# A copy ahead of the recurrent layer's gather, three places a step for the next chunks' stages, and a later final norm, in a four-layer graph network

## The chip, the cores and the metric

One core of a Trainium2 chip runs the whole kernel. Its engines are PE (TensorE: matrix products, with its weight loads shown apart as PEld), DVE (VectorE), ACT (ScalarE), POOL (GpSimd) and SP (SyncE, which issues nearly all transfers here). The metric is the device time of one execution in microseconds; less is better.

## The reference, cut to what matters

There are 128 graphs of 64 nodes with 256 features. Four layers follow one another, each as a residual and a layer norm over the features: `x = layernorm(x + layer(x))`.

- Layer 0 runs graph convolutions on five groups of the first 25 nodes.
- Layer 1 is one normalised graph convolution, layer 2 a polynomial of degree 3 in the row-normalised adjacency.
- Layer 3 is a gated recurrent unit that is stepped five times over the graph:

```python
A = (adj != 0).astype(x.dtype)
h = x
for l in range(5):
    m = einsum('bnd,de->bne', h, weight[l])
    agg = einsum('bij,bid->bjd', A, m)
    h = gru_cell(agg, h, w_ih, w_hh, b_ih, b_hh)
```

with `r` and `z` two sigmoid gates, `n = tanh(i_n + r * h_n)` and `h = (1 - z) * n + z * h`. All of it is float32. The change is in layer 3 and in how the work of layers 1 and 2 is laid between its steps.

## The kernel before, in words

The graphs are cut into 16 chunks of 8 graphs: four pairs of graphs, 128 rows each, so a chunk's state is 128 rows by 4 pairs by 256 features (`xt`), and transposed (`hT`, `hn`) 128 features by 2 halves by 512 nodes.

**Layer 3's main loop (L1011 to L1050)** has 80 steps, of which the last is written out by itself. Two chunks take turns: an even step belongs to one, an odd step to the other, and a chunk gets five steps, one for each application of the unit. Ten steps make a round of two chunks; the text counts them t=0 to t=9. There are eight rounds. In a step `x` is the chunk whose gates are computed and `w` is the other chunk, stepped just before. The order of PE's instructions is the order of the source (`manual_schedule` for PE alone). The other engines' orders are set by a scheduler from the dependencies, with `high_priority` for some instructions; each engine then works its list in order.

In a step PE computes the two big gates (r and z) in seven products `rz(1)` to `rz(7)`, and the candidate in seven products `n(1)` to `n(7)`; this is a product scheme of seven instead of eight (class `Gates`, L744 to L788). Each `rz` product is 8 instructions and each `n` product 4, in the lines of L759. Products 1, 6, 7 and 4 accumulate in one bank `a` (`parz`, `pan`); after 1, 6 and 7 ACT copies the bank to a tile `c` (L776), and the next product of the same bank waits for that copy. Products 5, 7 and 3 use a bank `d` (`pdrz`, `pdn`), and DVE adds `d` and a copy (L778, L788). The order in a step is: rz 1, 2, 6; filler; rz 5, 7; n 1, 2; rz 4; n 6; rz 3; n 5; filler; n 7; gather of `w`; n 4; n 3.

**The gather** (`messages`, L811, and `gather`, L206 to L215) multiplies, for each half k of the features, each pair's 128 by 128 state as the weights with the 0/1 adjacency `A01` as the moving operand, into a bank `pa`; ACT copies the bank to `agg` (L214), and POOL forms sums of it (`sums`, L736). For a chunk's first application the weights come from `xt`, where features are consecutive. For the four others they come from `h`.

**How `h` comes about** (`flip`, L862 to L880): DVE transposes each half of the new state in 32 by 32 blocks to a tile `flip` (L870), SP stores it to device memory (`hb`, L873) and loads it back in four transfers (L878) to `h`, a tile of 128 rows by 256 features by 4 pairs. The pair is the innermost index there, so consecutive features of one pair are 16 bytes apart: `src = lambda q, k: h[:, k * 128 : (k + 1) * 128, q]` (L815). `h` has one buffer.

**`close`** (L971 to L991): for `w` after its gather place, it counts the layer up and calls `messages`; after the fifth application it adds `h` to `xt` (DVE, L986), norms `xt` (DVE statistics, POOL power, ACT apply at L149) and stores it (SP, L991). When a chunk ends, a new chunk `nxt` is taken in: two transposes of its state (L800, L807) and its first gather.

**The filler** is the generator `mid` (L220 to L322), which computes layers 1 and 2 of the two chunks of the next round in stages. Each `next(filler)` runs one stage: S1 adjacency masks and sums (DVE); S2 four transposes (L259); S3 a product `pp` (L270), a gather `ag1` of 16 instructions and a second product (L278); S4 16 products `pd` with the layer-1 weights (L288) and statistics; S5 the norm (L152); S6 a gather `ag2`; S7 16 products with the layer-2 weights (L309), activation and statistics; S8 the norm. There are two places a step (L1027 after rz 6, L1041 after n 5), so the 16 stages of two chunks fill t=0 to t=7.

Of the kernel before, what the change touches and what calls it, by code (L numbers as in the profile page):

```python
# [9 lines left out]
F32 = mybir.dt.float32  # L10
# [5 lines left out]
B, N, D, HID, L = 128, 64, 256, 512, 5  # L16
# [9 lines left out]
H = CB * N // 2  # L26
NCH = B // CB
NP = CB // 2
# [40 lines left out]
def gnn_stack(  # L69
# [26 lines left out]
    nc = tc.nc  # L96
# [57 lines left out]
    def layernorm(y, by="v", n=NP, r=128):  # L154
        norm_apply(y, *norm_stats(y, by, n, r), by, n, r)
# [20 lines left out]
    def psum(name):  # L176
        return pt.tile([128, 512], F32, tag="pt", name=name)

    def psum0(name):

        taken[0] += 1
        if taken[0] % 8 < 5:
            return pg.tile([128, 512], F32, tag="pg", name=name)
        return psum(name)


    def load_adj(c):
        a64 = keep.tile([128, NP, N], F32, name="a64", bufs=2)
        nc.sync.dma_start(a64, av[c])
        adjs[c] = a64  # L190
# [11 lines left out]
    def halves(x):  # L202

        return lambda q, k: x[:, q, k * 128 : (k + 1) * 128]

    def gather(src, m, name, pool=keep, tag="ag", bufs=1):  # L206

        a = pool.tile([128, 2, NP * 128], F32, tag=tag, name=name, bufs=bufs)
        for k in range(2):
            p = psum("pa")  # L210
            for q in range(NP):
                nc.tensor.matmul(p[:, q * 128 : (q + 1) * 128], src(q, k), m[:, q, :], start=True, stop=True)  # L212
            with tc.high_priority():
                nc.scalar.copy(a[:, k, :], p)  # L214
        return a  # L215
# [1 line left out]
    adjs, xts = {}, {}  # L217
    state = {}

    def mid(c):  # L220

        a64 = adjs.pop(c)

# [33 lines left out]
        p = psum("pT1").rearrange("p (q n) -> p q n", q=NP)  # L257
# [10 lines left out]
        p = psum("pp").rearrange("p (q n) -> p q n", q=NP)  # L268
# [3 lines left out]
        with tc.high_priority():  # L272
            nc.vector.scalar_tensor_tensor(poly, dg, cw[:, 1:2], p, op0=ALU.mult, op1=ALU.add)
        ag = gather(halves(xt), AT1, "ag1")
        nc.vector.tensor_add(xt, xt, l1bs[:, None, :].to_broadcast([128, NP, D]))
        p = psum("pp").rearrange("p (q n) -> p q n", q=NP)
        for q in range(NP):
# [5 lines left out]
        for u in range(NP // 2):  # L283
            p = psum("pd").rearrange("p (q d) -> p q d", q=2)
            for h in range(2):
                q = 2 * u + h
# [4 lines left out]
            for h in range(2):  # L291
                q = 2 * u + h
# [11 lines left out]
        for u in range(NP // 2):  # L304
            p = psum("pd").rearrange("p (q d) -> p q d", q=2)
            for h in range(2):
                q = 2 * u + h
# [5 lines left out]
            for h in range(2):  # L313
                q = 2 * u + h
# [9 lines left out]
    def both(*gens):  # L324
        for g in gens:
            yield from g
# [8 lines left out]
    with ExitStack() as c0:  # L335
        w0 = c0.enter_context(tc.tile_pool(name="w0", bufs=1))
        work = c0.enter_context(tc.tile_pool(name="work0", bufs=1))
# [216 lines left out]
        p = psum0("pw")  # L554
# [27 lines left out]
                    )  # L582
            return p

        early = both(mid(0), mid(1))

        places = [(1, 1), (1, 2), (2, 1), (2, 2), (2, 2), (3, 1), (3, 2), (3, 2)]
        places += [(4, 0), (4, 0), (4, 1), (4, 2), (4, 2), (5, 1), (5, 2), (5, 2)]
# [105 lines left out]
    work = ctx.enter_context(tc.tile_pool(name="work", bufs=1, reuse_waits="tile"))  # L694
# [41 lines left out]
    def sums(a, name):  # L736

        t = work.tile([128, 4, H], F32, tag="T" + name, name="T" + name, bufs=2)
        nc.gpsimd.tensor_sub(t[:, 0:2, :], a[:, :, H:], a[:, 0, :].rearrange("p (s n) -> p s n", s=2))  # L739
        nc.gpsimd.tensor_sub(t[:, 2, :], a[:, 1, H:], t[:, 0, :])  # L740
        nc.gpsimd.tensor_sub(t[:, 3, :], a[:, 1, :H], t[:, 2, :])
        return t

    class Gates:  # L744
# [22 lines left out]
        def product(self, i):  # L767
            C = self.C
            if i == 1:
                self.a = self.bank("a")  # L770
            if i in (1, 6, 7, 4):
                self.multiply(self.a, i)
                if i != 4:
                    c = self.copies[i] = work.tile([128, 2, H], F32, tag="copy", name=f"c{i}", bufs=4)
                    with tc.high_priority():
                        nc.scalar.copy(c, self.a)  # L776
                if i == 7:
                    nc.vector.tensor_add(C[:, :, 1, H:], self.d, self.copies.pop(7))  # L778
            elif i == 2:
                b = self.bank("b")  # L780
                self.multiply(b, i)
                nc.vector.tensor_add(C[:, :, 0, :H], b, self.copies.pop(1))
            else:
                if i == 5:
                    self.d = self.bank("d")
                self.multiply(self.d, i)
                if i == 3:
                    nc.vector.tensor_add(C[:, :, 0, H:], self.d, self.copies.pop(6))  # L788

    class Chunk:  # L790
# [20 lines left out]
        def messages(self):  # L811
            src = halves(self.xt)
            if self.l:
                h = self.h
                src = lambda q, k: h[:, k * 128 : (k + 1) * 128, q]  # L815
            self.agg = gather(src, self.A01, "agg", work, "agg", 2)
            self.ta = sums(self.agg, "a")

# [43 lines left out]
        def flip(self, j):  # L862

            if self.c == NCH - 2 and self.l == L - 1:
                return
            if j:
                self.hb = dram.tile([2, 128, NP * 128], F32, name="hb", bufs=2)
            with tc.high_priority():
                t = work.tile([128, NP, 32, NP], F32, name="flip", bufs=2)
                nc.vector.transpose(  # L870
                    t.rearrange("p r f q -> p q r f"), self.hn[:, j, :].rearrange("p (q r f) -> p q r f", q=NP, r=NP)
                )
                nc.sync.dma_start(self.hb[j], t.rearrange("p r f q -> p (r f q)"))  # L873
                if not j:
                    self.h = work.tile([128, D, NP], F32, name="h", bufs=1)
                    hv = self.hb.rearrange("j (a i) (r c) -> r i (j a) c", i=32, r=NP)
                    for r in range(NP):
                        nc.sync.dma_start(  # L878
                            self.h[32 * r : 32 * (r + 1)].rearrange("p (a f) q -> p a (f q)", f=32), hv[r]
                        )  # L880

        def reset(self, j, f, i, h):
            n, r = self.NI[:, 1], self.RZ[:, 0]
            nc.vector.scalar_tensor_tensor(n[:, j, f], h, bhh[:, 4 + j : 5 + j], r[:, j, f], op0=ALU.add, op1=ALU.mult)  # L884
            nc.vector.tensor_add(n[:, j, f], i, n[:, j, f])  # L885
# [83 lines left out]
                )  # L969

        def close(self, norm=None):  # L971
            self.l += 1
            if self.l < L:
                self.messages()
                return
            if norm:
                mv, rs, _ = norm
                nb = small.tile([128, NP], F32, name="nb")
                nc.vector.scalar_tensor_tensor(nb, mv[:, :, 0], -1.0, rs, op0=ALU.mult, op1=ALU.mult)
                with tc.issue_after(tanhs[-1].ins):  # L980
                    norm_apply(self.xt, mv, rs, nb, "a")
            else:
                for q in range(NP):
                    m = self.c * NP + q
                    y = self.xt[:, q, :]
                    nc.vector.scalar_tensor_tensor(  # L986
                        y, self.h[:, :, q], mask[:, m : m + 1], y, op0=ALU.mult, op1=ALU.add
                    )
                layernorm(self.xt, "a")
            for h in range(2):  # L990
                nc.sync.dma_start(ov[self.c][:, 2 * h : 2 * h + 2], self.xt[:, 2 * h : 2 * h + 2])  # L991
# [4 lines left out]
    rows = []  # L996
# [13 lines left out]
    filler = iter(())  # L1010
    for s in range(NCH * L):  # L1011
        u, t = s // (2 * L) * 2, s % (2 * L)
        if t == 0:
            for _ in filler:
                pass
            if u + 2 < NCH:
                for c in (u + 2, u + 3):
                    load_adj(c)
                    load_x(c)
                filler = both(mid(u + 2), mid(u + 3))  # L1020
        if s == NCH * L - 1:
            break
        x, w = rows[s % 2], before
        nxt = None
        for i in (1, 2, 6):
            x.rz(i)
        next(filler, None)  # L1027
        x.rz(5)
        x.rz(7)
        x.n(1)  # L1030
        x.n(2)
        if w and w.l == L - 1 and w.c + 2 < NCH:
            nxt = Chunk(w.c + 2)
            nxt.state_of_layer2(1)
        x.rz(4)
        if nxt:
            nxt.state_of_layer2(0)
        x.n(6)
        x.rz(3)
        x.n(5)  # L1040
        next(filler, None)  # L1041
        x.n(7)
        if w:
            w.close()
            if nxt:
                nxt.messages()
                rows[(s + 1) % 2] = nxt
        x.n(4)
        x.n(3)
        before = x  # L1050

    x, w = rows[1], before
# [83 lines left out]
```

## Time and profile before

| what | value |
|---|---|
| median of three runs (lowest, highest) | 2286.38 us (2285.2, 2288.13) |
| the profiled execution's own time | 2285.78 us |
| its span in the trace | 2284.0 us |
| granted TensorE clock | 0.997 |
| PE busy | 2237.1 us, 98% of the span |
| weight loads busy | 1965.4 us, 86% |
| DVE, ACT, POOL busy | 1575.7, 953.2, 611.1 us |

The profiled execution is 2 us longer than its span, and 0.6 us under the median of the runs. Layer 3's loop takes the time from about 355 us to the end. PE is busy almost without a gap, so the time is the sum of PE's instructions plus a few waits. Engines other than PE matter where PE waits for them. Rows named L759 with tiles `parz`, `pan`, `pdrz`, `pdn`, `pbrz`, `pbn` are the gate products, rows L212 with `pa` the gathers. In a timeline, instructions of one line that follow each other are merged to one row with a count; a bracket names the idle time before it and what ended it.

### The profile page before, as it was taken

How to read it: one execution, taken by the hardware profiler on the slowest of the kernel's cores; microseconds unless marked ns; L12 is line 12 of the kernel's file. 1: busy time of each engine (PE TensorE's matmuls, PEld its weight loads, DVE VectorE, ACT ScalarE, POOL GpSimd, SP SyncE). 2: the span in 40 equal slices, each digit the busy share in tenths (PEclk: the TensorE clock that was granted, in tenths of full speed). 3: DMA queues.
4: the chain of work that ended last, by engine and by line, in shares of the span. 5: the costliest groups of instructions: out<-in, count | busy, mean ns of one | idle time of the engine just before them, and what ended most of it. 6: DMA issues, size and time to landing. Idle time of an engine off the chain costs nothing.

```text
span 2284.0 us, 29716 instructions
## 1 busy us (share of the span) xinstructions
PE 2237.1 (98%) x10914; PEld 1965.4 (86%) x10914; DVE 1575.7 (69%) x3133; ACT 953.2 (42%) x1718; POOL 611.1 (27%) x622
## 2 busy tenths in 40 slices
PE   9999999999999999999999999999999999998998
PEld 6777888889898988898888989898889888997997
DVE  3445757766877687676786686678777677666666
ACT  3333343434443444344443444344434443444444
POOL 3211132322322223222232232222222222222222
PEclk9999999999999999999999999999999999999999
DMA  6532011111211122112111121112211211112111
GB/s 166 176 105 87 25 35 40 42 44 47 77 46 47 40 72 61 40 38 74 58 44 42 47 76 49 47 37 74 58 37 42 70 47 47 47 37 68 44 57 37
DMA packets 161566, 132.91 MB, mean 58 GB/s; under 512 B 28431, under 2 KB 136461, under 8 KB 161421
## 3 DMA queue, kind: packets, MB, share of 16 engines
q1 hardware_dynamic: 156740, 125.77, 18.0%
q0 software_dynamic: 1968, 4.83, 0.8%
q8 instruction: 86, 1.41, 0.3%
q10 hardware_dynamic: 2712, 0.42, 0.1%
q14 instruction: 60, 0.48, 0.1%
HBM read 73.30 MB, written 57.67 MB: 57 GB/s over the span
## 4 chain that ended last, share of the span: by engine, by line
PE 80%; DVE 14%; DMA 2%; ACT 1%; issue 1%; POOL 1%; SPq 0%; ACTq 0%; POOLq 0%; DVEq 0%
PE parz L759 19%; PE pa L212 12%; PE pdrz L759 10%; PE pan L759 10%; PE pdn L759 5%; PE pbrz L759 4%; PE ps L460 4%; PE ph L444 4%; PE pbn L759 2%; PE pd L309 2%; PE pd L288 2%; DVE xt L986 1%; DVE flip L870 1%; DVE NI L884 1%; DMA h<-hb 1%
## 5 line engine op out<-in xcount | busy, mean ns | idle before, releaser
L759 PE MATMUL parz<-Th,WHH 128*128 128x256 f32 x960 | 287.2, 381 | 11.9 <-ACT c L776 11.9
L759 PE MATMUL parz<-Ta,V 128*128 128x256 f32 x960 | 285.8, 379 | 0.0
L776 ACT COPY c<-parz 128x512 f32<-128x512 f32 x240 | 140.1, 584 | 296.7 <-PE parz L759 296.7
L212 PEld LDWEIGHTS pa<-A,h 128*128 128x128 f32 x1024 | 243.8, 328 | 13.6 <-issue 7.7
L212 PE MATMUL pa<-A,h 128*128 128x128 f32 x1024 | 244.3, 393 | 9.2 <-DMA h<-hb 9.2
L739 POOL TENSOR_TENSOR Ta<-agg 128x512 f32<-128x512 f32 x80 | 104.7, 1308 | 548.2 <-ACT agg L214 548.2
L759 PEld LDWEIGHTS parz<-Th,WHH 128*128 128x128 f32 x960 | 180.1, 190 | 41.2 <-ACT c L776 18.1
L759 PEld LDWEIGHTS parz<-Ta,V 128*128 128x128 f32 x960 | 182.4, 190 | 24.8
L890 ACT ACTIVATE NI<-NI,bih 128x512 f32<-128x512 f32 x158 | 114.1, 722 | 212.3 <-DVE NI L885 212.3
L739 POOL TENSOR_TENSOR Th<-hn 128x512 f32<-128x512 f32 x64 | 87.0, 1360 | 408.7 <-DVE hn L893 378.0
L788 DVE TENSOR_TENSOR RZ<-pdrz,c 128x512 f32<-128x512 f32 x80 | 55.2, 691 | 204.2 <-PE pdrz L759 203.4
L137 POOL TENSOR_TENSOR rs<-ve,mhalf 128x4 f32<-128x4 f32 (+2 forms) x65 | 69.8, 1075 | 463.5 <-DVE ve L135 400.2
L870 DVE STREAM_TRANSPOSE flip<-hn 128x512 f32<-128x512 f32 x156 | 178.5, 1144 | 2.0
L214 ACT COPY agg<-pa 128x512 f32<-128x512 f32 x160 | 93.8, 586 | 168.6 <-PE pa L212 167.5
L776 ACT COPY c<-pan 128x512 f32<-128x512 f32 x237 | 138.1, 583 | 61.8 <-PE pan L759 58.0
L837 ACT ACTIVATE RZ<-RZ,brz 128x512 f32<-128x512 f32 x158 | 105.4, 714 | 134.4 <-DVE RZ L788 134.4
L759 PE MATMUL pan<-Ta,V 128*128 128x256 f32 x474 | 142.3, 382 | 0.7 <-ACT c L776 0.7
L759 PE MATMUL pan<-Th,WHH 128*128 128x256 f32 x474 | 141.6, 380 | 0.0
L778 DVE TENSOR_TENSOR NI<-pdn,c 128x512 f32<-128x512 f32 x79 | 54.5, 690 | 111.7 <-ACT c L776 111.7
L893 DVE TENSOR_TENSOR hn<-RZ,NI 128x512 f32<-128x512 f32 x158 | 108.9, 689 | 3.0
L884 DVE SCALAR_TENSOR_TENSOR NI<-NI,bhh,RZ 128x256 f32<-128x256 f32 (+1 forms) x158 | 107.8, 682 | 3.8
L892 DVE TENSOR_TENSOR RZ<-RZ 128x512 f32<-128x512 f32 x158 | 108.9, 689 | 0.3
(229 smaller groups left out, 4958.4 us busy)
## 6 DMA issues: line engine op xcount, KB each, us to landing
hb<-flip SPq DMA_DIRECT2D x156, 256.0 KB
h<-hb SPq DMA_DIRECT2D x312, 128.0 KB
out_dram<-xt SPq DMA_DIRECT2D x30, 256.0 KB
W<-in_w_dram SPq DMA_DIRECT2D x10, 512.0 KB
xt<-xb SPq DMA_DIRECT2D x32, 156.0 KB
xo<-in_x_dram SPq DMA_DIRECT2D x9, 512.0 KB
xb<-xo SPq DMA_DIRECT2D x9, 512.0 KB
xt<-xa SPq DMA_DIRECT2D x32, 100.0 KB
```

The lines of the kernel that those rows point to most:

```text
L212: nc.tensor.matmul(p[:, q * 128 : (q + 1) * 128], src(q, k), m[:, q, :], start=True, stop=True)
L214: nc.scalar.copy(a[:, k, :], p)
L444: nc.tensor.matmul(p, W1[:, u.g, k, e * 128 : (e + 1) * 128], ag0[:, k, : u.cols], start=k == 0, stop=k == 1)
L739: nc.gpsimd.tensor_sub(t[:, 0:2, :], a[:, :, H:], a[:, 0, :].rearrange("p (s n) -> p s n", s=2))
L759: nc.tensor.matmul(bank[:, g, :], w[:, q, i - 1, :], rhs, start=i in (1, 2, 5) and g == 0 and m == 0, stop=m == len(side) - 1, skip_group_ ...
L776: nc.scalar.copy(c, self.a)
L837: nc.scalar.activation(RZ[:, q, 0, :], RZ[:, q, 0, :], AF.Sigmoid, bias=b[0])
L870: nc.vector.transpose(t.rearrange("p r f q -> p q r f"), self.hn[:, j, :].rearrange("p (q r f) -> p q r f", q=NP, r=NP))
L884: nc.vector.scalar_tensor_tensor(n[:, j, f], h, bhh[:, 4 + j : 5 + j], r[:, j, f], op0=ALU.add, op1=ALU.mult)
L890: nc.scalar.activation(n, n, AF.Tanh, bias=bih[:, 4 + j : 5 + j])
L892: e.tensor_mul(d, d, z)
L893: e.tensor_add(self.hn[:, j, f], d, n)
```

## The change

- `rows` is new: for each half of the features ACT copies `h` to a tile `hk` of 128 rows by 4 pairs by 128 features, in which the features of a pair are consecutive. The gather of `w` reads `hk` in place of `h`. The copies may not stand ahead of the step's copy of the bank after n 6 on ACT (`issue_after(x.gn.copied)`).
- `hk` shares three buffers with `flip`, which had two of its own; the tiles `c` go from four buffers to three.
- `mid` has one more place to stop, between the gather `ag1` and the second `pp` product (not for the first two chunks), so there are 9 stages: S3 is cut to S3 and S3b.
- A third `next(filler)` a step, after n 1. The 18 stages of two chunks now fill t=0 to t=5.
- The final norm and the store of a chunk that ends are called after n 3, where they were called after n 7. What they compute is the same.

```diff
-    def mid(c):
+    def mid(c, first=False):
...
         ag = gather(halves(xt), AT1, "ag1")
+        if not first:
+            yield
         nc.vector.tensor_add(xt, xt, l1bs[:, None, :].to_broadcast([128, NP, D]))
...
-        early = both(mid(0), mid(1))
+        early = both(mid(0, True), mid(1, True))
...
-                    c = self.copies[i] = work.tile([128, 2, H], F32, tag="copy", name=f"c{i}", bufs=4)
+                    c = self.copies[i] = work.tile([128, 2, H], F32, tag="copy", name=f"c{i}", bufs=3)
                     with tc.high_priority():
-                        nc.scalar.copy(c, self.a)
+                        self.copied = nc.scalar.copy(c, self.a)
...
             if self.l:
-                h = self.h
-                src = lambda q, k: h[:, k * 128 : (k + 1) * 128, q]
+                hk = self.hk
+                src = lambda q, k: hk[k][:, q, :]
...
-                t = work.tile([128, NP, 32, NP], F32, name="flip", bufs=2)
+                t = work.tile([128, NP, 32, NP], F32, tag="flip", name="flip", bufs=3)
...
+        def rows(self, after):
+
+            self.hk = []
+            for k in range(2):
+                t = work.tile([128, NP, 128], F32, tag="flip", name="hk", bufs=3)
+                with tc.issue_after(after.ins):
+                    nc.scalar.copy(t, self.h[:, k * 128 : (k + 1) * 128, :].rearrange("p f q -> p q f"))
+                self.hk.append(t)
...
         def close(self, norm=None):
-            self.l += 1
-            if self.l < L:
-                self.messages()
-                return
...
         x.n(1)
+        next(filler, None)
         x.n(2)
...
         next(filler, None)
+        ended = w and w.l == L - 1
+        if w and not ended:
+            w.l += 1
+            w.rows(x.gn.copied)
         x.n(7)
-        if w:
-            w.close()
-            if nxt:
-                nxt.messages()
-                rows[(s + 1) % 2] = nxt
+        if nxt:
+            nxt.messages()
+            rows[(s + 1) % 2] = nxt
+        elif w and not ended:
+            w.messages()
         x.n(4)
         x.n(3)
+        if ended and s < NCH * L - 2:
+            w.close()
```

## Prediction

> **What bounds the kernel now.** I read the busy shares and the chain on the profile page first, then the groups by form, then the waits of PE, then a timeline of a plain step, then busy time over two steps. From the page:
>
> ```profile
> PE 2237.1 (98%) x10914; PEld 1965.4 (86%) x10914; DVE 1575.7 (69%) x3133; ACT 953.2 (42%) x1718; POOL 611.1 (27%) x622
> PE 80%; DVE 14%; DMA 2%; ACT 1%; issue 1%; POOL 1%; SPq 0%; ACTq 0%; POOLq 0%; DVEq 0%
> L212 PE MATMUL pa<-A,h 128*128 128x128 f32 x1024 | 244.3, 393 | 9.2 <-DMA h<-hb 9.2
> ```
>
> PE is busy for 98% of the span and holds 80% of the chain, so time falls if PE's instructions get shorter and nothing makes PE wait instead. The same gather on consecutive weights shows what is too long, in the groups by form:
>
> ```profile
> L212 PE MATMUL pa<-A,xt 128*128 128x128 f32 x256 | 31.2, 275 | 0.0
> ```
>
> The 1024 matmuls from `h` take 244.3 us of PE, so 16 take 3.8 us; 256 from `xt`, the same shape, take 31.2, so 16 take 1.95. In timelines one gather from `h` is one row of 3.79 us, one from `xt` a row of 1.95. Take one matmul's length off and divide by 15: a cadence of (3.79-0.393)/15 = 227 ns against (1.95-0.275)/15 = 112 ns. Layer 3 has 16 x 4 = 64 gathers from `h`, so 64 x 16 x 115 ns = **118 us** is the most that there is to gain. PE's waits, in us, times and longest:
>
> ```profile
> PE parz L759 <- ACT c L776: 11.9, 16, 1.1
> PE pp L278 <- DVE poly L273: 10.1, 13, 1.1
> PE pa L212 <- DMA h<-hb: 9.2, 7, 4.1
> ```
>
> They are small. What lies close behind PE is seen in the timeline of the end of a plain step (t=8 of a round; start, length, engine):
>
> ```profile
> 788.95 0.60 PE L759 MATMUL pdrz<-agg,V 128*128 128x256 f32 x2
> ...
> 789.59 0.69 DVE L788 TENSOR_TENSOR RZ<-pdrz,c 128x512 f32<-128x512 f32 x1 [3.56 <-PE pdrz L759]
> ...
> 790.31 1.33 ACT L837 ACTIVATE RZ<-RZ,brz 128x512 f32<-128x512 f32 x2 [1.81 <-DVE RZ L788]
> ...
> 790.68 0.59 PE L759 MATMUL pan<-Th,WHH 128*128 128x256 f32 x2
> ...
> 791.11 3.79 PE L212 MATMUL pa<-A,h 128*128 128x128 f32 x16
> 791.55 0.56 ACT L776 COPY c<-pan 128x512 f32<-128x512 f32 x1
> ...
> 794.74 0.60 PE L759 MATMUL pan<-Ta,V 128*128 128x256 f32 x2
> ```
>
> After rz 3 DVE adds, ACT makes two sigmoids, and behind them stands the copy `c` of n 7, which ends at 792.11. n 4 needs that copy, but the slow gather covers it until 794.74. Two stretches from one gather to the next, up to that of t=8 and from that of t=0 to that of t=1 (length; busy PE, PEld, DVE, ACT, POOL; clock, DMA share):
>
> ```profile
> 769.36:791.11 21.75, 21.75 (x101) 19.62 (x101) 13.94 (x21) 9.07 (x17) 5.79 (x6) 1.00 0.15 49
> 836.37:865.52 29.15, 27.37 (x149) 24.21 (x148) 27.79 (x63) 13.53 (x25) 8.35 (x8) 1.00 0.30 86
> ```
>
> A plain step leaves ACT more than half idle and DVE a third; around t=0 DVE is busy 27.79 of 29.15 us.
>
> **What the Trainium skill says.** Advanced Engine Details and Errata, section SBUF Cachelines: lines have 16 bytes, at least two hits on one are needed to hide the access, a new line for each element is penalised. Consecutive features of `h` are 16 bytes apart, and the trace agrees for PE: 227 against 112 ns. The copy on ACT reads with that same stride. Perfetto Trace Analysis, section Optimization Strategy, has one look for the gaps on the bounding engine and for the instruction that ends them; here these gaps are yet to be made, so I look for what would end them.
>
> **Part 1: gathers from `hk`.** 64 x 1.84 us shorter on PE: -118 us, if PE waits for nothing.
>
> **Part 2: 128 copies on ACT, 128x512 each, strided.** No row shows one. From below: a consecutive 128x512 takes 0.58 us from PSUM (L776) and 0.72 from SBUF (L890); ScalarE: Activation LUTs, Rules for kernel authors, gives about 0.3 us + 0.83 ns per element, 0.72 for 512. From above: PE's strided load costs 227/128 = 1.77 ns per element and DVE's strided L986 610/256 = 2.4 with its overhead (479 where consecutive); at PE's pace a copy costs 0.3 + 512 x 1.77 = 1.2. I take **1.1**, near the pace that both strided readers show, with 0.6 and 1.2 as ends. In all that is 141 us of ACT, 42% to 48% of the span: no bound by sum. What counts is where ACT does it.
>
> **Where it stands in ACT's list.** I compared the orders of the built programs. In t=6, 7 and 8 of every round, t=1 of rounds 2 to 7 and all of the last round (35 of 64 gathers), the two copies come after the copy `c` of n 7, and the gather follows n 7 on PE at once. So ACT does add, sigmoids, `c`, copy, copy in a row while PE stands. In t=2, 4, 5 and the first t=1 they come before the sigmoids; in t=3 after them and before `c`.
>
> *Late places, t=6 to 8.* With the shown lines: rz 3 ends 789.55, add to 790.28, sigmoids to 791.64, `c` to 792.22, first copy to 793.35 (1.1 and some 0.03 of handover). Half a gather now takes 8 x 112 ns = 0.9: 793.40 to 794.30. Second copy to 794.45, second half to 795.40. n 4 then starts at 795.40 against 794.74: **+0.66 us** per step, the saved 1.84 eaten by a wait of 2.5. At 0.72 a copy it is +0.08. Seven rounds x 3, and 7 steps of the last: 28 x 0.66 = **+18.5**.
>
> *t=4.* The copies follow n 6's and end about 790.7, before n 7 does: -1.84 x 7 = **-12.9**. What could go late next is `c` of n 7, behind the sigmoids until 792.2, and the gather now ends at 792.9: it holds.
>
> *t=3.* Copies follow the sigmoids; n 4 starts 7.45 us after n 6 where it took 8.21: -0.8 x 7 = **-5.6**.
>
> *t=2 and 5.* DVE's add after rz 3 now stands behind S7's statistics and S8's norm, which waits for POOL's power, so sigmoids and `c` are late; n 4 starts 5.05 after that add's place where it took 5.2: -0.15 x 14 = **-2**.
>
> **Part 3: three places a step.** The stages and their PE work are the same (S2 0.45, S3 with S3b 3.8, S4 3.45, S6 1.8, S7 3.45 us), only earlier, so PE's sum is unchanged. DVE's sum per round is too, about 201 us, but t=0 to t=5 now carry 21 to 22 us each. The transfers: `xt` loads of the next chunks go out at t=0, and two of them with two `out` stores stand on SP's queue between `hb` and `h`. Splitting S3 lets a wait for `poly` pass under other work: of 10.1 us, second chunks' 8 go: **-8**.
>
> **Part 4: the late norm.** At t=0 the norm and the `out` store of the closing chunk come after n 3, so DVE's work from one flip to the next is 30.6 us there against 25.9, by adding the row durations in DVE's order; in t=9 it is 18.2 against 20.7. POOL's power and ACT's apply move along, and the flip of t=0 starts later. Who waits: the gather of t=1, whose `h` comes 8.1 us after the flip (857.06 to 865.2 now). Before, from the end of n 3 in t=9 to that gather takes 48.5 us, 45.3 of work and 2.9 of waits, and it ends at 52.1. After, the flip ends at +42.5, `h` is there at 50.6, the first copy at 51.7, the gather ends about 54: +2 for each of rounds 2 to 7, **+12** (ends -3 and +5 each). The first round's t=1 gives -1.8, the last's -2.6 (its wait of 4.07 shrinks): **-4.4**.
>
> **Smaller edits.** `c` at three buffers: the copy of rz 1 is read out by 782.3, the taker begins at 784.4, 2.1 us of cover; nothing. `hk` with `flip` in three: `h` is refilled after ACT's copies rather than after PE's gather; it lands 15 us after n 3 in a plain step, while the copies are long done; nothing, but a late copy in t=0 would delay the reload.
>
> **Sum.** 18.5 - 12.9 - 5.6 - 2 - 8 + 12 - 4.4 = -2.4. The spacing from round to round is 246.4 us, of which the same bookkeeping explains 244.9; with more chains close behind PE I allow as much again, 1.5 x 8 = +12. On the profiled execution's 2285.8 (span 2284.0 and 2 outside; 0.6 under the median) this gives **2295**.
>
> **Rivals.**
> - *A, faster: the strided copy is cheap.* At 0.72 the 28 late steps give +2 rather than +18.5, t=1 some 5 less and t=3 5 less: about 2268. It decides below about 0.96 us per copy. For it: the skill's price has no stride term[...]. Against: both strided readers in the trace pay.
> - *B, slower still: DVE at t=0.* If the late norm and 30.6 us of DVE move t=0's flip 4 us more each round (8 x 4 less what t=9 returns) and the norm ahead of the add in t=2 and 5 costs 1 us: about 2325. For it: DVE's 27.79 of 29.15; against: t=9 is lightened by 2.5.
> - *C, the whole gain, 2168.* Only if copies never end late; ACT's order excludes it in 35 of 64.
> - *D, the gather isn't faster from `hk`* or the copies cost over 2 us: about 2400. The `xt` rows speak against it.
>
> **Chances.** A change within 0.2%, some 4.6 us, is what measurement can't tell from none. Forecast, 2281 to 2313: 0.50 (within 0.13, slower 0.35, faster 0.02). A 0.27, all faster. B 0.18 and D 0.02, slower. C 0.03. So faster 0.32, same 0.13, slower 0.55. Low 2256 (a copy of 0.6 gives some 8 below A, and t=1 at its lower end the rest), high 2326 for B; both signs are in it, and the likeliest case's own range is 2281 to 2313.
>
> **What would show it.** Gather rows from `hk` with a mean near 275 ns, 16 in about 1.95 (part 1). The ACT copy to `hk` at 1.0 to 1.2 us (part 2; at 0.72 rival A). A wait of PE's `pa` for ACT's `hk` of some 2.5 us in t=6 to 8 and none in t=4. The `pp` wait for `poly` down to about 2 us. The gather of t=1 waiting for `h` or `hk` (part 4), by over 6 us if B. If PE waits in t=4, or not in t=7, my reading of ACT's order is wrong.

## The result and the profile after

| | before | after |
|---|---|---|
| median (lowest, highest), 4 runs each | 2285.79 us (2284.31, 2288.13) | 2311.51 us (2310.63, 2312.71) |
| ratio to before, 95% interval | | 1.0112 (1.0094 to 1.0129) |
| span of the profiled execution | 2284.0 us | 2309.8 us |
| granted TensorE clock | 0.997 | 0.973 |

The change makes the kernel 25.7 us slower. The time lies in the range on record (2256 to 2326) and on the forecast side, but the loss is nearly three times the 9 us forecast. From the page of the changed kernel, the busy shares, the shares of the chain and the groups of the gather and of the new copies:

```profile
PE 2187.1 (95%) x10914; PEld 1887.3 (82%) x10914; DVE 1551.3 (67%) x3133; ACT 1073.3 (46%) x1846; POOL 582.9 (25%) x622
...
PE 74%; DVE 14%; ACT 8%; POOL 2%; issue 2%; DMA 1%; SPq 0%; ACTq 0%; POOLq 0%; DVEq 0%
...
L212 PE MATMUL pa<-A,hk 128*128 128x128 f32 x1024 | 162.5, 320 | 84.9 <-ACT hk L890 84.9
...
L890 ACT COPY hk<-h 128x512 f32<-128x512 f32 x128 | 137.9, 1122 | 2.6 <-DMA h<-hb 2.5
```

The gather's busy time falls by 244.3 - 162.5 = 81.8 us, and a copy costs 1.12 us, as forecast. But PE now idles 84.9 us ahead of the gathers, and ACT has 8% of the chain where it had 1%. The gather rows should have summed to 64 x 1.95 = 125 us; 320 ns is not the 275 of consecutive weights. PE's waits:

```profile
PE pa L212 <- ACT hk L890: 84.9, 43, 4.6
PE pan L761 <- ACT c L778: 12.0, 17, 0.8
PE parz L761 <- ACT c L778: 10.7, 15, 1.9
```

The wait for `poly` is gone, that for `h` has become one for `hk`, nine times as long. How a late step looks, from the timeline of t=7 of a round (start, length, engine), which answers to the plain step shown of before:

```profile
1012.50 0.59 PE L761 MATMUL pdrz<-agg,V 128*128 128x256 f32 x2
...
1013.13 0.69 DVE L790 TENSOR_TENSOR RZ<-pdrz,c 128x512 f32<-128x512 f32 x1 [3.56 <-PE pdrz L761]
...
1013.85 1.33 ACT L839 ACTIVATE RZ<-RZ,brz 128x512 f32<-128x512 f32 x2 [1.81 <-DVE RZ L790]
...
1014.22 0.59 PE L761 MATMUL pan<-Th,WHH 128*128 128x256 f32 x2
1015.09 0.56 ACT L778 COPY c<-pan 128x512 f32<-128x512 f32 x1
1015.56 2.14 ACT L890 COPY hk<-h 128x512 f32<-128x512 f32 x2
...
1016.71 3.12 PE L212 MATMUL pa<-A,hk 128*128 128x128 f32 x16 [1.89 <-ACT hk L890]
...
1019.62 1.06 PE L761 MATMUL pan<-Ta,V 128*128 128x256 f32 x2
```

The chain add, sigmoids, `c`, copies stands as the prediction wrote it. New is what follows the wait: the gather's row is 3.12 us long, not 2.2, and n 4's first two matmuls 1.06, not 0.60. The clock is lower there, by the busy times of five stretches around it (length; busy PE, PEld, DVE, ACT, POOL; then the clock that the throttle granted):

```profile
1014.00:1016.00 2.00, 0.82 (x4) 0.38 (x2) 0.31 (x1) 2.00 (x4) 0.00 (x0) 1.00 0.00 0
1016.00:1018.00 2.00, 1.29 (x9) 1.25 (x10) 1.29 (x3) 1.70 (x2) 0.00 (x0) 0.90 0.00 0
1018.00:1020.00 2.00, 2.00 (x9) 1.96 (x10) 0.13 (x1) 0.72 (x2) 0.00 (x0) 0.50 0.00 0
1020.00:1022.00 2.00, 2.00 (x8) 1.67 (x7) 0.88 (x3) 0.45 (x1) 1.40 (x2) 0.75 0.00 0
1022.00:1024.00 2.00, 2.00 (x11) 1.74 (x11) 1.97 (x4) 0.75 (x2) 1.33 (x2) 1.00 0.00 0
```

After a wait of 1.89 us PE runs at half its clock for 3.4 us. The fill below tests whether this, and not the wait by itself, is what costs. Over the span the clock's loss is 2309.8 x (1 - 0.973) = 62 us, against 2284.0 x 0.003 = 7 before.

The second new thing is in t=1. The timeline of the same round, in its second step, behind n 7:

```profile
864.02 0.59 PE L761 MATMUL pan<-Th,WHH 128*128 128x256 f32 x2
864.37 1.38 DVE L152 TENSOR_SCALAR xt<-xt,mv,rs 128x256 f32<-128x256 f32 x4 [1.12 <-POOL rs L137]
...
865.67 0.68 DVE L790 TENSOR_TENSOR RZ<-pdrz,c 128x512 f32<-128x512 f32 x1
866.38 1.33 ACT L839 ACTIVATE RZ<-RZ,brz 128x512 f32<-128x512 f32 x2 [4.54 <-DVE RZ L790]
867.62 0.56 ACT L778 COPY c<-pan 128x512 f32<-128x512 f32 x1
868.09 2.11 ACT L890 COPY hk<-h 128x512 f32<-128x512 f32 x2
...
869.25 3.78 PE L212 MATMUL pa<-A,hk 128*128 128x128 f32 x16 [4.63 <-ACT hk L890]
```

Here the norm of stage S5 (L152), which waits for POOL, stands ahead of the add after rz 3, and the add, the sigmoids, `c` and the copies follow in a row: 4.63 us of wait. `h` did not come late. In two stretches of half a microsecond (the DMA share is the last figure but one) the transfers end by 864.0, and n 7 ends at 864.61:

```profile
863.50:864.00 0.50, 0.50 (x4) 0.45 (x3) 0.00 (x0) 0.00 (x0) 0.50 (x1) 1.00 0.46 84
864.00:864.50 0.50, 0.50 (x3) 0.19 (x1) 0.13 (x1) 0.00 (x0) 0.33 (x1) 1.00 0.00 0
```

### The profile page after: what moved, and what is told of

It is laid out like the page before. It is cut to its first block, busy times and chain, and to the rows that moved or that the text cites. A ratio compares the mean times of both kernels' runs of the same rounds, so it can differ in the third digit from the quotient of the medians.

```text
span 2309.8 us, 29895 instructions
## 1 busy us (share of the span) xinstructions
PE 2187.1 (95%) x10914; PEld 1887.3 (82%) x10914; DVE 1551.3 (67%) x3133; ACT 1073.3 (46%) x1846; POOL 582.9 (25%) x622
## 3 DMA queue, kind: packets, MB, share of 16 engines
q8 instruction: 86, 1.41, 0.3%
## 4 chain that ended last, share of the span: by engine, by line
PE 74%; DVE 14%; ACT 8%; POOL 2%; issue 2%; DMA 1%; SPq 0%; ACTq 0%; POOLq 0%; DVEq 0%
PE parz L761 21%; PE pdrz L761 10%; PE pan L761 9%; PE pa L212 7%; PE pbrz L761 5%; PE ps L462 4%; PE ph L446 4%; PE pdn L761 3%; ACT RZ L839 3%; ACT hk L890 2%; PE pbn L761 2%; DVE st L132 2%; PE pd L290 2%; ACT c L778 2%; DVE RZ L790 2%
## 5 line engine op out<-in xcount | busy, mean ns | idle before, releaser
L212 PE MATMUL pa<-A,hk 128*128 128x128 f32 x1024 | 162.5, 320 | 84.9 <-ACT hk L890 84.9
L212 PEld LDWEIGHTS pa<-A,hk 128*128 128x128 f32 x1024 | 147.9, 223 | 106.1 <-ACT hk L890 103.2
L761 PE MATMUL pan<-Ta,V 128*128 128x256 f32 x474 | 156.1, 414 | 12.0 <-ACT c L778 12.0
L778 ACT COPY c<-pan 128x512 f32<-128x512 f32 x237 | 137.3, 580 | 43.6 <-PE pan L761 21.6
L761 PE MATMUL pan<-Th,WHH 128*128 128x256 f32 x474 | 151.7, 404 | 0.0
L890 ACT COPY hk<-h 128x512 f32<-128x512 f32 x128 | 137.9, 1122 | 2.6 <-DMA h<-hb 2.5
L895 DVE SCALAR_TENSOR_TENSOR NI<-pan,bhh,RZ 128x256 f32<-128x256 f32 x79 | 37.7, 478 | 119.3 <-PE pan L761 119.3
L837 ACT ACTIVATE RZ<-parz,brz 128x256 f32<-128x256 f32 x158 | 66.1, 468 | 104.9 <-PE parz L761 104.9
```

What stands on the lines that cost most here:

```text
L761: nc.tensor.matmul(bank[:, g, :], w[:, q, i - 1, :], rhs, start=i in (1, 2, 5) and g == 0 and m == 0, stop=m == len(side) - 1, skip_group_ ...
L778: self.copied = nc.scalar.copy(c, self.a)
L890: nc.scalar.copy(t, self.h[:, k * 128 : (k + 1) * 128, :].rearrange("p f q -> p q f"))
```

## The experiments

**The clock: fill the wait with idle work.** PE is given matmuls whose result is overwritten, first eight calls, then four. The expectations speak of the clock's grid: the halved stretches begin only at points 3.41 us apart, as the last section works out.

```diff
             p = psum("pa")
+            for i in range(0 if k else fill):
+                nc.tensor.matmul(p[:, :256], ident, L1W[:, 0, :], start=True, stop=True)
...
-            w.messages()
+            w.messages(8 if t in (6, 7, 8) or u + 2 == NCH else 0)
```

> The changed kernel with eight further matmuls (128x128 by 128x256, the identity and a layer weight, into the gather's bank, overwritten by the gather) between the last gate product before the gather and the gather, in t=6, 7, 8 of each round and in all steps of the last round: 28 places, 8 x 0.217 = 1.7 us of idle work in a wait of 1.90 us. Theory 1 (each wait of 1.90 us that falls into one window of the clock's grid halves PE's clock for 3.4 us, 1.71 us of PE lost; 21 of the 28 places have such a drop, 36 us in all): the clock stays at 1.00 there, gather rows of 3.1 us become 2.2, and the time falls by 30 to 36 us to about 2278, with more work on PE. Theory 2 (the waits themselves and the slower rows behind them come from the ACT copies: the gather reads hk while ACT writes and starts cold): nothing of this changes, 2311 or a little more.

Measured 2304.42 us (2303.84 to 2305.8; ratio 1.0078, 1.0063 to 1.0093): a miss of both. In the trace the clock stays at 1.00 in all 28 places (the edit also fills t=1 of the last round, a 29th). But the fill is 16 matmuls of 3.45 us in all, since a float32 call makes two: it is 1.5 us longer than the wait, and a step of 23.37 us is bound by it.

> The fill again with four matmul calls in place of eight, since the trace showed that each call is two passes: 8 x 0.216 = 1.73 us of idle work in the wait of 1.90 us, in the same 28 places. In the run with eight, a late step took 23.37 us with 3.45 us of fill and no halved clock, so 23.37 - 1.72 = 21.65 and a remaining wait of up to 0.2 are expected here against 22.3, 23.1, 23.85 in the changed kernel's t=6, 7, 8 and 23.88 in the last round. Theory 1 (the halved clock is what the wait costs beyond its own length): 2304.4 - 28 x 1.6 = about 2260, up to 2268. Theory 2 (the wait and the restart cost it, not the clock): about 2311.

Measured 2274.22 us (2273.42 to 2275.01; ratio 0.9948, 0.9934 to 0.9963). **37 us are gained by giving PE more to do.** In t=7 of a round, after 1.7 us of fill:

```profile
1010.60 2.15 ACT L892 COPY hk<-h 128x512 f32<-128x512 f32 x2
...
1011.77 2.19 PE L214 MATMUL pa<-A,hk 128*128 128x128 f32 x16 [0.19 <-ACT hk L892]
...
1013.80 0.60 PE L763 MATMUL pan<-Ta,V 128*128 128x256 f32 x2
```

The copies end as late as ever after n 7, but the gather takes 2.19 us and n 4 is at its 0.60 again. A step takes 22.25 us against 21.76 before the change: +0.49, which is the prediction's late step of +0.66 as it would be at full clock. I had expected 21.65 and 2260; the step is bound by the copies' end, which a fill can't move. Theory 2 falls.

**ACT's order: copies, then `c`, then the sigmoids.** Nothing needs the two sigmoids after rz 3 before n 3.

```diff
-                elif i == 3:
-                    nc.scalar.activation(RZ[:, q, 0, :], RZ[:, q, 0, :], AF.Sigmoid, bias=b[0])
+        def late_sigmoids(self, after):
+            with tc.issue_after(after.ins):
+                for q in range(2):
+                    v = self.RZ[:, q, 0, :]
+                    nc.scalar.activation(v, v, AF.Sigmoid, bias=brz[:, 2 * q : 2 * q + 1])
...
-                with tc.issue_after(after.ins):
-                    nc.scalar.copy(t, ...)
+                with tc.issue_after(after.ins), tc.high_priority():
+                    after = nc.scalar.copy(t, ...)
...
-            w.rows(x.gn.copied)
+            x.gn.behind = w.rows(x.gn.copied)
         x.n(7)
+        x.late_sigmoids(x.gn.copied)
```

(`behind` holds the copy `c` of n 7 behind the second copy.)

> The changed kernel with only ACT's order changed: copies of h first, then the copy c of n 7, then the two sigmoids after rz 3, which nothing needs before n 3. Theory 1 (the slowdown is ACT's order, copies that end late and the clock drops behind them): in t=6 to 8 h lands some 1.5 us before n 7 ends, so PE waits 0 to 0.3 us there and no clock drops: each of 28 late steps gives back 2.1 and gains 1.8, with a few more us from t=2, 3, 5; about 2190 to 2215. Rival (the three places a step and the late norm are what costs; the copies' order only matters a little): 2290 to 2305.

Measured 2194.25 us (2192.38 to 2196.58; ratio 0.9592, 0.9576 to 0.9608): 117 us less than the change as it was, at a clock of 0.995. Of waits for `hk` more is left than I expected, 39.3 us in 35 places. In t=1, where the change waited 4.63 us:

```profile
836.02 0.59 PE L762 MATMUL pan<-Th,WHH 128*128 128x256 f32 x2
836.60 2.13 ACT L900 COPY hk<-h 128x512 f32<-128x512 f32 x2 [2.76 <-DMA h<-hb]
836.93 0.68 DVE L795 TENSOR_TENSOR RZ<-pdrz,c 128x512 f32<-128x512 f32 x1
...
837.76 2.17 PE L212 MATMUL pa<-A,hk 128*128 128x128 f32 x16 [1.15 <-ACT hk L900]
838.62 0.58 ACT L781 COPY c<-pan 128x512 f32<-128x512 f32 x1
839.10 0.73 ACT L849 ACTIVATE RZ<-RZ,brz 128x512 f32<-128x512 f32 x1
```

The copy now starts when `h` lands, and DVE's late add no longer stands ahead of it. To see where that gain lies, the same edit was made in some steps alone, t=1 and then t=6 and later with the last round (the diff shows one line of it):

```diff
+        if t == 1:
             x.late_sigmoids(x.gn.copied)
```

> The changed kernel with ACT's order changed (copies, c of n 7, sigmoids) in t=1 alone. Theory (the 4.6 us wait of t=1 is DVE's add after rz 3 standing behind the norm S5, with sigmoids, c and the copies in a row behind it, while h has long landed): the wait falls to 1 us or less in rounds 2 to 7, the step from 32.7 to some 26 us: about 2272 to 2280. Rival, the forecast's step (h comes late, because the flip of t=0 does): the wait stays near 4 us and the time near 2311.

Measured 2277.53 us (2274.36 to 2280.84; ratio 0.9964, 0.9952 to 0.9975): -34. Six waits are left in t=1, 7.4 us in all; the longest is 1.8, where 1 or less was expected.

> The changed kernel with ACT's order changed (copies, c of n 7, sigmoids) in t=6 to 9 of each round and in the last round alone, the other part of the order experiment. From the step times of the changed kernel and of the one with the order changed everywhere: t=6 to 9 take 90.8 us and 84.5, seven times, and a step of the last round 23.9 and 21.3, seven times: 2311.5 - 44 - 18 = about 2250. If the parts don't add (the clock's grid moves), 2240 to 2270.

Measured 2246.35 us (2244.7 to 2248.93; ratio 0.9825, 0.9808 to 0.9842): -65. If the parts add, that and -34 leave 117 - 99 = 18 us for t=2 to 5.

**The parts by themselves.** The copies alone, on the kernel before:

```diff
+        if w and w.l < L - 1:
+            w.rows(x.gn.copied)
         x.n(7)
```

> The kernel before with the copies and the gather from hk alone (two places a step, S3 whole, norm after n 7; buffers as in the changed kernel). Theory 1: late copies behind the copy c of n 7 make PE wait 1.9 us in some 35 to 45 gathers with a clock drop in most of them, so this is slower than before too: about 2310 to 2330. Rival (stages and norm cost): about 2290 or below.

Measured 2293.89 us (2283.6 to 2300.51 in 20 runs; ratio 1.0034, 1.0027 to 1.0042): slower, by 8 us and not by 25 to 45. The waits are there, 78.3 us in 48 gathers, but fewer of them halve the clock (0.987): 14 times in the loop of its trace, against 28 times in that of the change. The runs spread over 17 us, where four of the changed kernel lie within 2, and the run of 2283.6 has a clock of 0.991, that of 2295.9 one of 0.986. Without copies:

```diff
-            w.rows(x.gn.copied)
```

> The changed kernel without the copies: the gather reads h itself, the three places, S3 cut in two and the late norm stay. Theory 1: no late copies and no clock drops but perhaps at t=1; my forecast's terms for these parts are +12 for t=0 and 1, -8 for the poly wait: 2280 to 2300. Rival (stages and norm cost): about 2311.

Measured 2269.15 us (2266.95 to 2270.92; ratio 0.9922, 0.9907 to 0.9937), below what I expected: the stages and the norm gain 16.5 us where the prediction had about nothing. So within the change the copies cost 2311.5 - 2269.2 = 42 us.

```diff
         x.n(7)
+        if ended and s < NCH * L - 2:
+            w.close()
...
         x.n(3)
-        if ended and s < NCH * L - 2:
-            w.close()
```

> The kernel without copies, with three places and S3 cut, but the final norm called after n 7 again as before. The kernel with the late norm took 2269. If the gain of these parts is the poly wait alone (10 of 16.5 us), the norm gives the rest: about 2275. If the late norm costs time at t=0, as my forecast had it: 2255 to 2262. If the norm's place is nothing: 2269.

Measured 2281.09 us (2279.15 to 2283.73; ratio 0.998, 0.9971 to 0.9989): the late norm gains 12 of the 16.5 us, more than any of my three cases had. PE's wait for `h`, first with the late norm and then with the early one:

```profile
PE pa L212 <- DMA h<-hb: 4.3, 4, 1.5
```

```profile
PE pa L212 <- DMA h<-hb: 21.1, 8, 4.1
```

So the earlier stages by themselves do make `h` late, 21.1 us of wait where the kernel before has 9.2, and the late norm takes this away again.

**The price of the stride.**

```diff
-    self.h[:, k * 128 : (k + 1) * 128, :].rearrange("p f q -> p q f")
+    self.h[:, k * 128 : (k + 1) * 128, :].rearrange("p (q f) r -> p q (f r)", q=NP)
```

> The changed kernel with the copies reading h in consecutive order (the gather then works on features and pairs in another order, so it leaves out the reordering). Forecast for the copy: 0.72 us against 1.12, since the stride of 16 bytes is what it pays. Theory 1: PE's wait in t=6 to 8 falls from 1.90 to 1.5; if 1.5 us still halves the clock, the time falls by some 0.55 x 28 + a few = about 2290, if it doesn't, to about 2262. Rival (the stride costs ACT nothing): the copy stays at 1.1 and the time at 2311.

This kernel leaves out the reordering, so it does not compute the reference's result; it is used for its times alone. Measured 2251.99 us (2249.02 to 2254.54; ratio 0.9851, 0.9836 to 0.9865). The group of the copies:

```profile
L890 ACT COPY hk<-h 128x512 f32<-128x512 f32 x128 | 73.7, 619 | 4.4 <-DMA h<-hb 4.3
```

The stride makes a copy of 0.62 us one of 1.12. Of the 28 late waits 26 are 1.41 us long, and the clock stays at 1.00 behind every one of them; the other two are 2.19 and 2.73 us long, and it halves behind both. A late step without a halved clock takes 21.6 us. So half a microsecond per copy decided over the clock in the late places. In t=1 it did not: the wait there is still 4.1 us in five rounds.

**A version that beats both.** With the order changed everywhere, PE's waits are those for `h` and the first copy. In t=6 and later and in the last round DVE takes two of the four pairs:

```diff
+                n = 2 if added else NP
                 with tc.issue_after(after.ins), tc.high_priority():
-                    after = nc.scalar.copy(t, src)
+                    after = nc.scalar.copy(t[:, :n], src[:, :n])
+                if added:
+                    with tc.issue_after(added.ins), tc.high_priority():
+                        added = nc.vector.tensor_copy(t[:, n:], src[:, n:])
```

> The kernel with the order changed everywhere, and in t=6 to 9 and the last round DVE copies two of the four pairs of each half, ACT the other two, so that a half is in place after one copy of 128x256 (some 0.6 us) rather than one of 128x512 (1.12). PE's wait of 0.7 to 1.1 us there falls to 0.2 to 0.6 and the second half no longer waits; 28 places by 0.5 to 0.8 us: 2194 - 14 to 22 = 2172 to 2180. If DVE's part makes the sum for n 7 or the flip late: no gain, 2190 to 2200.

Measured 2175.99 us (2175.83 to 2178.11; ratio 0.952, 0.9506 to 0.9534): 110 us under the kernel before. PE's longest groups of waits, which for `hk` were 39.3 us with ACT alone:

```profile
PE pa L212 <- ACT hk L902: 28.5, 36, 2.5
PE parz L762 <- ACT c L783: 3.5, 7, 0.5
```

## Why the prediction was right and wrong

Step times (n 4 to n 4) of the third round show where the change differs from its own parts without the copies:

| us | t=0 | t=1 | t=2, 3 | t=4 | t=5 | t=6 | t=7 | t=8 | t=9 | sum |
|---|---|---|---|---|---|---|---|---|---|---|
| changed | 24.38 | 32.70 | 50.73 | 24.60 | 26.06 | 22.31 | 23.10 | 23.79 | 21.54 | 249.21 |
| without copies | 24.38 | 28.12 | 51.98 | 26.10 | 27.00 | 21.75 | 21.76 | 21.81 | 20.80 | 243.70 |

- **Gather and copy: right.** Consecutive weights make the gather 1.95 us, and a copy takes 1.12 (1.1 taken). Rivals A and D fall with that: the stride does cost ACT half a microsecond, and the gather is faster. Rival C falls with the late copies.
- **Late places, t=6 to 8: the order was right, the cost was not.** t=6 is +0.55 against "+0.66"; t=7 and 8 are +1.34 and +2.0, and t=9 still pays 0.7 for a halved clock that began in t=8. In the last round a step takes 23.88 us, +2.1. The step of the working that failed is "the saved 1.84 eaten by a wait of 2.5": it priced a wait at its own length. The wait is shorter than I wrote, 1.90 and some 0.2 more for the second copy, but behind 21 of the 28 PE works at half clock. By the step times of the two traces the late places cost 44 us in all, where "+18.5" was written. Filling the wait gave 37 us back; this is the largest term that the forecast lacked.
- **t=1: the wrong chain.** "The flip ends at +42.5, `h` is there at 50.6, the first copy at 51.7": in the trace, counted alike from the end of n 3 at 817.64, the flip ends at +39.0 and `h` has landed when n 7 ends at +47.0. What came last was DVE's add behind the norm. I had seen this for t=2 and 5 ("now stands behind S7's statistics and S8's norm") and not for t=1, where S5's norm stands likewise, although I counted t=1 among the late places. It costs 4.6 us in the round of the table and 23 in all eight; the order changed in t=1 alone gave 34 us. Rival B had its place, t=0 and t=1, and in most rounds nearly its size, but not its cause: the flip of t=0 is not later than before (+39.0 against +39.6).
- **The late norm: the wrong sign.** I let 30.6 us of DVE work stand between the flips where 25.9 stood. That sum of row durations comes true, 30.5 in the trace, but rows overlap: from flip to flip it takes 28.2 us (828.45 to 856.64) where it took 25.3, so 2.9 more and not 4.7. And the flip of t=9 comes 3.5 us earlier against n 3, not 2.5, since the norm of the chunk before no longer stands ahead of it. So the flip of t=0 is not late, and the late norm gains 12 us, where "+12" was written.
- **The `poly` wait: right in kind.** Its 10.1 us are gone, against the 8 forecast; with the early norm the kernel gains only 5 us by the stages, since the wait for `h` grows meanwhile.
- **t=2 to 5: right in sum.** -20.5 forecast for 28 places; -3.7 a round measured, about -26 for seven. t=4 gains 1.5 of the 1.84, t=5 gains 0.9 where next to nothing was written.
- **The allowance of 12** for small waits was there to cover such things and covered less than half. Of the parts, the copies cost 42 us rather than about 0, and the stages and the norm gained 16.5: two errors of opposite sign. That the time still lies in the range on record is in part luck.
- **Slips in the working.** `L986` was read at 610 ns; the median in the trace of before is 675. The stretch of 48.5 us is 48.2 by its own parts, 45.3 and 2.9. The 0.72 us for a consecutive 128x512 on ACT is that of an activation with a bias (L890); a copy takes 0.62. None of these carries the error.

The part of the clock is shown by the fill, the part of t=1 by the order. Why the copies alone lose less can be read from their trace, by the grid of the last section. In their last round seven waits of 1.90 us lie each within one interval of the grid and all halve the clock, and a step takes up to 23.87 us, as in the change. In the seven rounds before there are 29 waits of over 1.5 us: 17 run over a grid line, 6 of 1.73 or 1.74 us lie within one interval and leave the clock as it was, and 6 halve it. No run shifted these waits on the grid by itself.

## What to carry to other kernels

A wait on the bounding engine is not priced by its length alone: ask what the clock does behind it, and read the granted clock of the stretch after it. Work that is put on a half-idle engine costs its place in that engine's list: look for what stands ahead of it with a late input, and for what could go behind it, here two sigmoids that nothing needed for a while. And trace each place where a moved stage lands ahead of a short instruction that someone waits for, not only the first two that come to mind.

## What the runs showed of the hardware

- **The clock halves on a grid.** In the changed kernel the half clock begins at 1017.6, 1041.5 and 1116.6, distances of 7 and 22 times 3.41 us, and lasts 3.4 us, or 6.8 after a wait of 4.63. The wait of t=7 (1014.8 to 1016.7) lies in one interval of that grid and halves the clock of the next; the equally long one of t=6 (992.6 to 994.5) is cut by a grid line at 993.7, and the clock stays. It is so for all 28 late waits of 1.90 us in this trace: 21 lie within one interval and halve the clock of the next, the 7 of t=6 in the first seven rounds are cut and don't. In the last round the steps settle at 23.88 us = 7 x 3.41, so that each wait falls alike.
- The Trainium skill, TensorE: Matmul & The Clock Gate, Part 1: The HAM clock gate, has the free-running window of 3.4 us, and the trace agrees; it has the clock fall after an idle window, and here 1.90 us of idling within one were enough. Waits of 1.73 to 1.75 us within one interval were in 3 of 9 cases of the copies alone, waits of 1.41 us in none of 27 with the consecutive copies.
- A float32 matmul call makes two matmuls of the trace: eight calls of 128x256 are 16 in the trace and took 3.45 us.
